# The last block of a graph-attention layer: offset, scale row and store queues at the end of the kernel

## Chip, cores and metric

One core of one Trainium2 chip. The metric is the device time of one execution in microseconds (us). A trace gives the profiled span as well, which is about 1.8 us shorter than the timed figure of the same execution. Lower is better. Engines: PE is TensorE (matmuls), DVE is VectorE, ACT is ScalarE, POOL is GpSimd, SP is SyncE, which here only issues transfers (DMA).

## The reference, cut to what matters

```python
# x: (128, 64, 768) f32, adj: (128, 64, 64); two layers l; H = 768
h = max(layernorm(x), 0)
for l in range(2):
    ...                                   # scores, exp, mask -> attention (64 x 64 for each of 128 graphs)
    h_lin = h @ W_lin[l].T + b_lin[l]
    ctx   = attention @ h_lin
    h     = relu((ctx - mean) / (std + 1e-3) * ln_a[l] + ln_b[l])
out = x + h
```

The change concerns the last line of the loop for l = 1 and the residual `x + h`, for the last sixteenth of the rows. The kernel has the mean taken out of `h_lin` beforehand, so that `ctx` comes centred and the deviation is the root of the sum of its squares.

## The kernel before: the parts concerned

The kernel makes four passes, two a layer. Each goes over 16 blocks of 512 rows. In the last pass a block's product with `W_lin` (15 groups of matmuls with `ts`/`ht` tiles; each group's PSUM bank, called X, Y, Z or V, is read out and added into `hl`: an *eviction*) is followed, in two halves, by the *context* matmuls (`attention @ h_lin`, into PSUM tiles `aux`) and by `finish`. A half r = 0 or 1 has two tiles k = 0, 1 of 128 rows and 768 columns. In the last block the halves of the product also run one after the other, so that the first half is finished while PE works on the second. `put(slot, f)` places the steps among the matmul groups; each engine has its instructions in a fixed order.

```python
def finish(u, r):                                        # (cut to the last pass)
    cx = context(u, r)                                   # PE: 8 context matmuls, 16 records
    ...
    for k in range(2):
        nc.scalar.activation(zs[k], cx[k], AF.Square, accum_out=ss[:, k:k + 1])
    nc.scalar.activation(sd, ss, AF.Sqrt, bias=floor, scale=1.0 / (H - 1.0))

    def inverse():                                       # 1 / (deviation + eps), both tiles at once
        nc.vector.tensor_scalar_add(rs, sd, EPS_LN)
        nc.vector.reciprocal(rs, rs)
    def scaled(k):
        nc.vector.scalar_tensor_tensor(zs[k], cx[k], rs[:, k:k + 1], rows["a"], op0=ALU.mult, op1=ALU.mult)
        nc.gpsimd.tensor_add(zs[k], zs[k], rows["b"])
    def done(k):
        nc.vector.scalar_tensor_tensor(xs[k], zs[k], 0.0, xs[k], op0=ALU.max, op1=ALU.add)
        for h in range(PAIR):
            nc.sync.dma_start(out[...], xs[k][...])      # two stores of 192 KB
        if k and (u < NB - 1 or r == 0):
            residual(u + r, 1 - r)                       # loads the next rows of x, just in time
...
# last block: the block before it is finished in these slots, then its own first half
linear(u, (0,), 0, {0: ((u - 1, 0), (12, 13, 15, 19, 21)), 11: ((u - 1, 1), (34, 35, 36, 42, 44))}, (1,))
linear(u, (1,), 30, {4: ((u, 0), (50, 51, 52, 56, 58))}, ())
for f in finish(u, 1):                                   # the last half: nothing beside it
    f()
```

Of the kernel before, what the change touches and what calls it, by code (L numbers as in the profile page):

```python
# [10 lines left out]
F32 = mybir.dt.float32  # L11
I32 = mybir.dt.int32
AF = mybir.ActivationFunctionType
# [4 lines left out]
def kernel(  # L18
# [58 lines left out]
    def put(slot, *fs):  # L77
        plan.setdefault(slot, []).extend(fs)
# [96 lines left out]
    def put_sums_t(key, first, step, base):  # L175

        fs = sums_t(key)
        put_all(first, fs[:5], step)
        for f, s in zip(fs[5:], (21, 22, 23, 24, 25, 27)):
            put(max(base + s, first + 5 * step), f)  # L180
# [346 lines left out]
    def pass_two(l, aside):  # L527
        last = l == L - 1
        with tc.tile_pool(name=f"two{l}", bufs=2, reuse_waits="tile") as sp:
            if last:  # L530
                for name, src in (("a", ln_a), ("b", ln_b)):
                    row(name, src[l], 0, H, sp.tile([P, H], F32, name=name, bufs=1))
            AT, HL = {}, {}

            def load(u):
                if (2, l, u) not in HT:
                    load_h(2, l, u)
                AT[u] = sp.tile([P, Q, S], F32, name="at", bufs=3)
                nc.sync.dma_start(AT[u], ATT[l][u])

            def context(u, r):


                hl, at = HL[u], AT[u]
                lo, hi = slice(0, S), slice(S, P)
                cx = [ps_aux.tile([P, 2, T], F32, name="aux") for _ in range(2)]
                for n in range(2):
                    for (j, k, i) in ((lo, 0, lo), (hi, 0, hi), (lo, 1, hi), (hi, 1, lo)):
                        q = r + 2 * k
                        m = n if j == lo else 1 - n  # L550
                        nc.tensor.matmul(cx[k][i, m, :HH], at[j, q, :], hl[j, q, m * HH:(m + 1) * HH],  # L551
                                         start=True, stop=True)
                return [c[:, :, :HH] for c in cx]

            def batch(r, k, h):
                return 4 * (h if k == 0 else 1 - h) + r + 2 * k

            XS = {}

            def residual(u, r):  # L560
                XS[u, r] = [sp.tile([P, H], F32, name="xr", bufs=4) for _ in range(2)]
                for k in range(2):
                    for h in range(PAIR):
                        nc.sync.dma_start(XS[u, r][k][h * S:(h + 1) * S], x[u * NBB + batch(r, k, h)])

            def finish(u, r):

                cx = context(u, r)
                zs = [sp.tile([P, H], F32, name="z", bufs=4 if last else 3) for _ in range(2)]
                if last and not u and not r:  # L570
                    residual(u, r)
                two = "p (n d) -> p n d"
                ss = stat.tile([P, 2], F32, name="ss")
                sd = stat.tile([P, 2], F32, name="sd1")
                rs = stat.tile([P, 2], F32, name="rs1")
                for k in range(2):
                    nc.scalar.activation(zs[k].rearrange(two, n=2), cx[k], AF.Square, accum_out=ss[:, k:k + 1])

                nc.scalar.activation(sd, ss, AF.Sqrt, bias=floor, scale=1.0 / (H - 1.0))

                def inverse():
# [4 lines that stand above are left out]
                    if last:  # L586
                        nc.vector.scalar_tensor_tensor(  # L587
                            zs[k].rearrange(two, n=2), cx[k], rs[:, k:k + 1],
                            rows["a"].rearrange(two, n=2), op0=ALU.mult, op1=ALU.mult)
                        nc.gpsimd.tensor_add(zs[k], zs[k], rows["b"])  # L590
                        return
                    nc.scalar.activation(zs[k].rearrange(two, n=2), cx[k], AF.Copy, scale=rs[:, k:k + 1])
                    for h in range(PAIR):
                        nc.sync.dma_start(ROWS[u][batch(r, k, h)], zs[k][h * S:(h + 1) * S])

                def done(k):
                    if last:
                        xs = XS[u, r]
                        nc.vector.scalar_tensor_tensor(xs[k], zs[k], 0.0, xs[k], op0=ALU.max, op1=ALU.add)
                        for h in range(PAIR):  # L600
                            nc.sync.dma_start(out[u * NBB + batch(r, k, h)], xs[k][h * S:(h + 1) * S])
                        if k and (u < NB - 1 or r == 0):
                            residual(u + r, 1 - r)

                return [inverse] + [lambda k=k: scaled(k) for k in range(2)] + [lambda k=k: done(k) for k in range(2)]

            def linear(u, rs, base, ends, more):

                b, w = tokens_of((2, l, u)), W[l, "n"]
                if rs[0] == 0:  # L610
                    HL[u] = sp.tile([P, Q, H], F32, name="hl", bufs=2)
                hl, seen = HL[u], set()
                bank = {"X": AHEAD.pop()}
                early = {0: 3, 2: 5, 6: 9}
                for i, (s, at, t, _) in enumerate(ORDER):
                    if i in FIRST and i not in PRELOAD:
                        bank[at] = fresh(l, i, rs)
                    p = bank[at]
                    for n, r in enumerate(rs):
                        for c in range(K2):  # L620
                            nc.tensor.matmul(p[:, n], b[t][:, c, r * P:(r + 1) * P], w[s][:, c, :],  # L621
                                             start=(i in FIRST and i not in PRELOAD and n == c == 0),
                                             stop=(c == K2 - 1), skip_group_check=True)
                        if n == 0:
                            run(base + 2 * i)
                    read(p, lambda o: hl[:, o % 2 * 2 + rs[0]:o % 2 * 2 + rs[0] + len(rs), o // 2 * D:(o // 2 + 1) * D],
                         i, seen)
                    if i in early:
                        bank[FIRST[early[i]][0]] = fresh(l, early[i], rs)
                    if i == 11 and more:  # L630
                        AHEAD.append(fresh(l, 0, more))
                    if i in ends:
                        what, slots = ends[i]
                        for f, n in zip(finish(*what), slots):
                            put(n, f)
                    run(base + 2 * i + 1)

            load(0)
            for u in range(NB):
                turn = not last and u >= NB - 2  # L640
                if u + 1 < NB:
                    load(u + 1)
                    put_all(9 if u else 15, affine(2, l, u + 1))
                    put_sums_t((2, l, u + 1), 15 if u else 21, 1, 0)
                    if turn:
                        load_rows(1, 0, sp)
                        put_all(10, transpose_rows(1, 0, sp), 2)
                    if u in aside:
                        aside[u]()
                    ends = {}  # L650
                    if u:
                        ends = {0: ((u - 1, 0), (6, 7, 8, 11, 12)), 7: ((u - 1, 1), (20, 21, 22, 30, 30))}
                    linear(u, (0, 1), 0, ends, (0, 1) if u + 2 < NB else (0,))
                    for n in sorted(plan):
                        plan[n - 30] = plan.pop(n)
                else:
                    if turn:
                        load_h(1, 1, 0)
                        put_all(22, affine(1, 1, 0))
                        put_sums_t((1, 1, 0), 30, 2, 30)  # L660
                    linear(u, (0,), 0, {0: ((u - 1, 0), (12, 13, 15, 19, 21)),
                                        11: ((u - 1, 1), (34, 35, 36, 42, 44))}, (1,))
                    linear(u, (1,), 30, {4: ((u, 0), (50, 51, 52, 56, 58))}, ())
                    for n in sorted(plan):
                        run(n)
                    for f in finish(u, 1):
                        f()

    def one_aside(l):
# [46 lines left out]
```

## Time and profile before

| | |
|---|---|
| timed, 4 runs | 2812.39 us median (2810.76 to 2813.75) |
| profiled span | 2811.2 us |
| PE busy over the span | 98% |
| PE idle at the end | the last 13 us |

The lines are in the prediction below. In a timeline line the columns are start and length in us, engine, source line, operation, what it writes and reads, shapes, how many equal instructions in a row it merges, and, in brackets, the idle time of the engine just before and what ended it. SPq and ACTq are DMA issues from those engines' queues, whose data arrive later. PE's records overlap, so only their starts are used here.

For what follows I measure three stretches on each trace, by instructions that every version has:

- **C**: start of the second context group of the block before the last (2771.50 before).
- **A**: start of the last block's first context group (2780.05 before).
- **T**: start of the first square of the last half (2797.49 before).

### The profile page before, as it was taken

The numbers are of one execution on the slowest core, as the hardware profiler recorded it, in microseconds if no ns is written. First come the engines' busy times: TensorE is split into PE (matmuls) and PEld (weight loads), VectorE is DVE, ScalarE is ACT, GpSimd is POOL, SyncE is SP. The second block draws the span as 40 slices with busy tenths as digits, with TensorE's granted clock in tenths as the row PEclk, the third lists the DMA queues.
The fourth block names the chain that finished last, engine by engine and source line by source line (L and its number), as shares of the span: only waits on it lengthen the run. The fifth ranks groups of instructions, "written<-read, shape, count | busy, mean of one in ns | idle before, by whom it ended". The sixth has DMA issues, their size and how long they took to land.

```text
span 2811.2 us, 46104 instructions
## 1 busy us (share of the span) xinstructions
PE 2755.9 (98%) x18712; PEld 2343.6 (83%) x18712; DVE 1338.1 (48%) x2222; ACT 838.0 (30%) x1453; POOL 1189.7 (42%) x935
## 2 busy tenths in 40 slices
PE   7999999999999999999999999999999999999997
PEld 6888888888888888888778888888888888888885
DVE  6455554454444332322334434443444335666666
ACT  2122222322231244444422121112111214545443
POOL 3343333223323455565423343223322335887875
PEclk9999999999999999999999999999999999999999
DMA  5632443234322243333563432343234304555654
GB/s 156 165 76 74 100 116 78 74 96 120 79 73 76 98 159 110 99 125 105 148 159 84 119 92 74 83 117 94 74 80 118 75 25 145 159 170 160 184 161 124
DMA packets 234068, 310.80 MB, mean 111 GB/s; under 512 B 54144, under 2 KB 184448, under 8 KB 225664
## 3 DMA queue, kind: packets, MB, share of 16 engines
q1 hardware_dynamic: 233568, 307.06, 39.9%
q8 instruction: 149, 2.44, 0.4%
q10 hardware_dynamic: 288, 0.79, 0.1%
q14 instruction: 63, 0.52, 0.1%
HBM read 202.91 MB, written 104.86 MB: 109 GB/s over the span
## 4 chain that ended last, share of the span: by engine, by line
PE 94%; DVE 2%; issue 1%; DMA 1%; POOL 1%; ACT 1%; SPq 0%; DVEq 0%; ACTq 0%; POOLq 0%
PE X L356 23%; PE V L356 15%; PE X L621 12%; PE Y L356 11%; PE Z L356 8%; PE V L621 8%; PE Y L621 6%; PE aux L382 5%; PE Z L621 4%; PE aux L551 3%; POOL w_r L144 1%; DVE m L144 0%; DMA z<-z 0%; DVE wm L396 0%; DMA x<-in_x_dram 0%
## 5 line engine op out<-in xcount | busy, mean ns | idle before, releaser
L144 POOL TENSOR_TENSOR ts<-ht 128x512 f32<-128x512 f32 x441 | 585.5, 1339 | 1249.1 <-DMA ht<-h 560.8
L189 ACT ACTIVATE m<-X 128x512 f32<-128x512 f32 x256 | 152.3, 595 | 1117.8 <-PE X L356 585.9
L144 POOL TENSOR_TENSOR ts<-ht,ts 128x512 f32<-128x512 f32 x189 | 248.8, 1324 | 155.4 <-PE X L621 78.2
L144 DVE TENSOR_TENSOR m<-m,V 128x512 f32<-128x512 f32 x256 | 174.2, 681 | 272.0 <-PE V L356 272.0
L144 DVE TENSOR_TENSOR m<-m,X 128x512 f32<-128x512 f32 x256 | 163.8, 681 | 252.0 <-PE X L356 251.4
L356 PE MATMUL X<-ts,w_l 128*128 128x256 f32 x1024 | 246.6, 384 | 10.7 <-ACT m L189 5.1
L621 PE MATMUL X<-w_n,ts 128*128 128x256 f32 x1024 | 245.1, 381 | 6.0 <-ACT hl L189 5.7
L356 PE MATMUL X<-ts,w_r 128*128 128x256 f32 x1024 | 241.9, 379 | 0.0
L144 DVE TENSOR_TENSOR m<-m,Z 128x512 f32<-128x512 f32 x128 | 88.0, 688 | 322.7 <-ACT m L189 254.4
L356 PEld LDWEIGHTS X<-ts,w_l 128*128 128x128 f32 x1024 | 194.1, 192 | 43.0 <-issue 6.0
L621 PEld LDWEIGHTS X<-w_n,ts 128*128 128x128 f32 x1024 | 192.0, 190 | 37.6 <-ACT hl L189 6.3
L356 PEld LDWEIGHTS X<-ts,w_r 128*128 128x128 f32 x1024 | 192.3, 190 | 28.7
L255 ACT ACTIVATE ht<-ht,b_col,a_col 128x512 f32<-128x512 f32 x192 | 143.1, 804 | 149.2 <-DMA ht<-h 149.2
L621 PE MATMUL Y<-w_n,ts 128*128 128x256 f32 x768 | 182.9, 380 | 0.0
L356 PE MATMUL Y<-ts,w_l 128*128 128x256 f32 x768 | 181.8, 380 | 0.0
L356 PE MATMUL Y<-ts,w_r 128*128 128x256 f32 x768 | 181.4, 379 | 0.0
L189 ACT ACTIVATE hl<-X 128x512 f32<-128x512 f32 (+1 forms) x136 | 77.7, 571 | 332.8 <-PE X L621 323.2
L621 PEld LDWEIGHTS Y<-w_n,ts 128*128 128x128 f32 x768 | 146.5, 191 | 20.1
L356 PEld LDWEIGHTS Y<-ts,w_l 128*128 128x128 f32 x768 | 146.4, 191 | 20.1
L356 PEld LDWEIGHTS Y<-ts,w_r 128*128 128x128 f32 x768 | 145.9, 190 | 19.8
L590 POOL TENSOR_TENSOR z<-z,b 128x768 f32<-128x768 f32 x64 | 115.4, 1814 | 95.4 <-DVE z L587 95.4
L144 DVE TENSOR_TENSOR hl<-hl,X 128x512 f32<-128x512 f32 (+1 forms) x136 | 83.2, 653 | 146.2 <-PE X L621 144.3
(105 smaller groups left out, 4680.7 us busy)
## 6 DMA issues: line engine op xcount, KB each, us to landing
ht<-h SPq DMA_DIRECT2D x63, 1536.0 KB, 7.2
h<-xb SPq DMA_DIRECT2D x124, 384.0 KB, 6.5
z<-z SPq DMA_DIRECT2D x128, 192.0 KB, 2.8
x<-z SPq DMA_DIRECT2D x128, 192.0 KB, 8.6
xr<-in_x_dram SPq DMA_DIRECT2D x128, 192.0 KB, 3.8
out_dram<-xr SPq DMA_DIRECT2D x128, 192.0 KB, 2.6
x<-in_x_dram SPq DMA_DIRECT2D x120, 192.0 KB, 8.5
adj<-in_adj_dram SPq DMA_DIRECT2D x64, 128.0 KB, 2.7
```

The costliest lines, as they stand in the source:

```text
L144: (eng.tensor_add if sign == "+" else eng.tensor_sub)(o, a, b)
L189: nc.scalar.activation(to(o), p, AF.Copy, scale=1.0 if sign == "+" else -1.0)
L255: nc.scalar.activation(ht, ht, AF.Relu, bias=cols[1][:, c:c + 1], scale=cols[0][:, c:c + 1])
L356: nc.tensor.matmul(p[:, g], w[ORDER[i][0]][:, c, g * P:(g + 1) * P], b()[t][:, c, :], start=(new and g == c == 0), stop=(c == K2 - 1), ski ...
L382: nc.tensor.matmul(p[h * S + e:h * S + e + 32, q, e:e + 96], ht[:, c, b * S + e:b * S + e + 32], mb[:, e:e + 96], start=(c == 0), stop=(c ...
L551: nc.tensor.matmul(cx[k][i, m, :HH], at[j, q, :], hl[j, q, m * HH:(m + 1) * HH], start=True, stop=True)
L590: nc.gpsimd.tensor_add(zs[k], zs[k], rows["b"])
L621: nc.tensor.matmul(p[:, n], b[t][:, c, r * P:(r + 1) * P], w[s][:, c, :], start=(i in FIRST and i not in PRELOAD and n == c == 0), stop=(c ...
```

## The change

Intent: shorten the chain after the last matmul. relu(z·a + b) + x is rewritten as max(z·a, -b) + (x + b). The x + b is made ahead of time on GpSimd, for rows loaded early into a spare tile (*advance adds*); the multiplication by a goes ahead of the root; the maximum takes -b; the offset's GpSimd step falls away; each tile has its own root; and the last half's stores go out on two queues. Line numbers move by 52: the residual add L599 is L651 in the new file for older blocks, the offset L590 is L642, the scale L587 is L639; the new steps are L577 (advance add), L590 (square), L592 (root), L595 (scale row), L599 to L601 (eps, reciprocal, multiply and maximum), L604 (residual add) and L606 (store).

```diff
+            def last_block(u):
+                rest = big.tile([P, C, T], F32, name="ht")...           # spare tile, cut into four row tiles
+                rows["-b"] = sp.tile([P, H], F32, name="nb", bufs=1)
+                ...
+                put(1, lambda: load(0))
+                put(2, lambda: load(1))
+                put(6, lambda: nc.gpsimd.tensor_scalar_mul(rows["-b"], rows["b"], -1.0))
+                for n, slot in enumerate((23, 26, 45, 49)):
+                    put(slot, lambda xs=XS[u, n // 2][n % 2]: nc.gpsimd.tensor_add(xs, xs, rows["b"]))
+            def finish_last(u, r):
+                ...
+                for k in range(2):                                      # square and root by tile
+                    nc.scalar.activation(XS["squares"][...], cx[k], AF.Square, accum_out=ss)
+                    nc.scalar.activation(rs[k], ss, AF.Sqrt, bias=floor, scale=1.0 / (H - 1.0))
+                def gained(k):
+                    nc.vector.tensor_tensor(zs[k], cx[k], rows["a"], op=ALU.mult)
+                def scaled(k):
+                    nc.vector.tensor_scalar_add(rs[k], rs[k], EPS_LN)
+                    nc.vector.reciprocal(rs[k], rs[k])
+                    nc.vector.scalar_tensor_tensor(zs[k], zs[k], rs[k], rows["-b"], op0=ALU.mult, op1=ALU.max)
+                def done(k):
+                    nc.vector.tensor_add(xs[k], xs[k], zs[k])
+                    for h in range(PAIR):
+                        (nc.scalar if r and h else nc.sync).dma_start(out[...], xs[k][...])
+                return [gained 0, gained 1, scaled 0, done 0, scaled 1, done 1]      # abridged
...
-                        if k and (u < NB - 1 or r == 0):
+                        if k and (u < NB - 2 or r == 0):
...
+                    else:
+                        last_block(u)
...
-                    linear(u, (1,), 30, {4: ((u, 0), (50, 51, 52, 56, 58))}, ())
+                    linear(u, (1,), 30, {4: ((u, 0), (41, 43, 47, 51, 53, 56) if last else (50, 51, 52, 56, 58))}, ())
-                    for f in finish(u, 1):
+                    for f in (finish_last if last else finish)(u, 1):
```

## The prediction

> **What bounds the kernel now.** I read the page first: TensorE (PE) is busy in 98% of the span, and the chain of work that ended last lies on it for 94%.
>
> ```profile
> span 2811.2 us, 46104 instructions
> PE 2755.9 (98%) x18712; PEld 2343.6 (83%) x18712; DVE 1338.1 (48%) x2222; ACT 838.0 (30%) x1453; POOL 1189.7 (42%) x935
> ...
> PE 94%; DVE 2%; issue 1%; DMA 1%; POOL 1%; ACT 1%; SPq 0%; DVEq 0%; ACTq 0%; POOLq 0%
> ```
>
> The diff touches only the last of 16 blocks of the last pass, and the order of the built program agrees: PE has the same instructions in the same order, and the other engines differ only in their last few dozen. So at most the stretch from about 2759 us to the end can change, 52 us of 2811. Then I read the table of windows, for how far PE still runs there (columns: window, its length, busy time of PE, weight loads, VectorE (DVE), ScalarE (ACT), GpSimd (POOL), then PE's clock, DMA share, GB/s):
>
> ```profile
> 2759.00:2775.00 16.00, 15.89 (x90) 11.28 (x90) 13.36 (x20) 6.81 (x19) 10.16 (x7) 1.00 0.48 124
> 2775.00:2788.00 13.00, 12.95 (x66) 9.65 (x65) 7.34 (x16) 5.50 (x16) 3.59 (x2) 1.00 0.50 134
> 2788.00:2799.00 11.00, 8.02 (x32) 3.86 (x30) 6.43 (x10) 1.51 (x4) 3.58 (x2) 0.84 0.62 179
> 2799.00:2811.20 12.20, 0.00 (x0) 0.00 (x0) 5.69 (x6) 0.48 (x3) 3.56 (x2) 0.59 0.42 119
> ```
>
> PE is full to 2788, has holes to 2799, and does nothing in the last 12.2 us. Those 12.2 us and the holes are all there is to win. The timeline from 2788 on, by engine, shows what fills them:
>
> ```profile
> 2787.17 3.43 SPq L564 DMA_DIRECT2D xr<-in_x_dram  x4
> 2788.70 1.94 DVE L587 SCALAR_TENSOR_TENSOR z<-aux,rs,a 128x768 f32<-128x768 f32 x2
> 2792.61 1.64 DVE L599 SCALAR_TENSOR_TENSOR xr<-z,xr 128x768 f32<-128x768 f32 x1 [1.32 <-DMA xr<-in_x_dram]
> 2794.17 0.41 DVE L144 TENSOR_TENSOR hl<-hl,Z 128x256 f32<-128x256 f32 x1
> 2794.64 3.59 PE L551 MATMUL aux<-hl,at 64*64 64x384 f32 x14 [1.37 <-DVE hl L144]
> 2797.49 0.81 ACT L577 ACTIVATE z<-aux 128x768 f32<-128x768 f32 x1 [12.05 <-PE aux L551]
> 2799.21 0.30 ACT L579 ACTIVATE sd<-ss,floor 128x2 f32<-128x2 f32 x1
> 2799.54 0.17 DVE L582 TENSOR_SCALAR rs<-sd 128x2 f32<-128x2 f32 x1 [3.76 <-ACT sd L579]
> 2800.03 1.94 DVE L587 SCALAR_TENSOR_TENSOR z<-aux,rs,a 128x768 f32<-128x768 f32 x2
> 2801.19 3.56 POOL L590 TENSOR_TENSOR z<-z,b 128x768 f32<-128x768 f32 x2 [7.76 <-DVE z L587]
> 2803.03 3.41 DVE L599 SCALAR_TENSOR_TENSOR xr<-z,xr 128x768 f32<-128x768 f32 x2 [1.06 <-POOL z L590]
> 2805.59 2.42 SPq L601 DMA_DIRECT2D out_dram<-xr  x4
> ```
>
> To see: at 2792.6 the residual add of the first row-half had waited for its late load, then ran 1.64 us, and the two eviction adds that PE's last matmuls need (L144) stood behind it on DVE. After the last matmul everything is serial: squares, root, DVE scale, GpSimd offset, DVE max-add, four stores on one queue.
>
> **What the Trainium skill says.** (1) "SBUF — State Buffer", Who interferes with whom: a DVE instruction with two SBUF inputs and a GpSimd one that reads SBUF exclude each other for the whole instruction. The trace agrees. Alone, an L599 takes 0.95 us (at 2772.92); beside a GpSimd add
>
> ```profile
> 2767.94 3.58 POOL L590 TENSOR_TENSOR z<-z,b 128x768 f32<-128x768 f32 x2 [2.36 <-DVE z L587]
> 2769.91 2.42 DVE L599 SCALAR_TENSOR_TENSOR xr<-z,xr 128x768 f32<-128x768 f32 x1
> ```
>
> it takes 2.42, ending 0.81 after the add's end at 2771.52: it waited, then ran. L587, with one input in PSUM, stays at 1.01. (2) "PSUM — Partial Sum Buffer", PSUM bank collisions: two engines may not be on one bank at once, ScalarE and VectorE reads included. The built program agrees: the new scale multiplication waits for ScalarE's square of the same tile, so "beside" means beside the square of the other tile. (3) "DMA: Bandwidth & Descriptors", Issuing engines are not separate DMA queues: a second issuing engine saves only issue time. Here one store occupies SP for 0.54 us, 2.42 for four; no run yet shows the saving. (4) "TensorE: Matmul & The Clock Gate", What's actually happening: PE's clock halves after a mostly idle window of 3.4 us. The windows above show it falling to 0.84 and 0.59, and the 14 context matmul records at 2794.64 took 3.59 us where 16 took 1.52 at 2771.50.
>
> **The change, part by part.** Call T the start of the first square of the last row-half (2797.49 now).
>
> Now: two squares with their accumulator reads end at T+1.69, root to T+2.02, add and reciprocal to T+2.4, first scale T+2.54 to 3.56, first GpSimd offset T+3.70 to 5.50 (1.81 each), then L599 waits for the lock behind the second offset and ends at T+8.08 instead of about T+6.5. Stores issue at T+8.10 and each 0.62 after; the last at about T+9.98. The span ends at T+13.71, so 3.73 us (landing, 2.8 by the issue list, and closing barriers) follow the last issue.
>
> After: square 0 with its accumulator read ends at T+0.90 and its root at 1.23; square 1 starts about 1.15 and ends with its read at 2.08. The multiplication by the scale row is a tensor-tensor: 0.416 for 256 columns and 0.683 for 512 give about 0.95 for 768. It runs at T+0.95 to 1.9 for tile 0, and, held by square 1, T+2.13 to 3.08 for tile 1. Add and reciprocal take 0.48 to the start of what follows (2799.54 to 2800.03); the multiply-max, two SBUF inputs, 0.95 as an undisturbed L599: T+3.48 to 4.43. Residual add T+4.47 to 5.42, then two stores at once, on SP and on ACT. Tile 1: add and reciprocal T+5.33, multiply-max T+5.82 to 6.77, add to T+7.75, two stores at T+7.8. Plus 3.73: **T+11.5, a gain of 2.2 us**. The offset is off the path, the lock costs nothing as GpSimd is finished, and the store queue saves one issue (0.6); against it stands one more pass of DVE per tile (0.95 each).
>
> **What T does.** DVE gets more to do before T, for the first row-half is treated the same way while PE is still running: per tile three wide DVE passes in place of two, and two small ones more in all, about 2.3 us together. And GpSimd's four advance adds (1.81 each, the first two queued behind the offsets ending at 2771.52, the others behind those ending at 2783.48) fall where DVE does residual adds for the block before. By working down the DVE order with the alternating lock:
> - The second residual add, 2772.92 now, would wait for the first advance add (2772.25 to 2774.05) and end at 2774.9, not 2773.87. The eviction behind it gates a matmul at 2774.78 with 0.25 of slack: PE loses about **0.8**.
> - Around 2784 DVE has, ahead of the eviction that releases PE's group at 2786.79, two new scale multiplications (0.9 each) and two residual adds that now meet the third and fourth advance adds. The present slack is 0.44. That PE group starts near 2790.2, so **2.6 beyond the 0.8**.
> - Gained back: no wait for a load at 2792.6 (1.32), no lock there (0.7), and no pair of L587 ahead of the evictions at 2790.5 (1.94). On my count the last eviction ends at about 2796.7 to 2797.2, against 2795.78 now; if PE is at full clock then, the context group's remainder takes about 0.9 instead of 1.7, and T becomes about 2798.1: **0.6 later**.
>
> Sum: -2.2 + 0.6 = -1.6 us. Without the collisions T would be near 2795.9 and the sum -3.8; with PE at half clock at the end too, -0.9.
>
> **The rivals.** A: the advance adds cost nothing, because their loads land after the residual adds have the lock, or the lock falls more kindly; gain near 3.8, so 2809. For it: loads here land 3.8 us after issue and eight are queued at once. Against: GpSimd is idle after its offsets, and DVE is busy 13.36 of 16 us there. B: DVE becomes the bound of the last block, T moves by 2 or more, and nothing is left: 2812 to 2813. For it: the slack of 0.25 and 0.44, and a cold PE. Against: the three waits that vanish. C: the second queue does not shorten the end, since both feed the same engines and 3.73 us of landing stay: costs 0.6 of the gain. Nothing makes 2%: that is 56 us, more than the 52 touched.
>
> **Range and chances.** The timed median is 1.5 above the profiled span (2812.73 to 2811.2), and the three runs spread over 1.7. I carry the shift over. My count gives 2811.1, rival A 2809; I weigh them two to one and say **2810.4 us**, range **2808.2 to 2812.6**: A's full gain plus noise below, B's almost nothing above. Faster by 2%: 0.004; within 2%: 0.992; slower: 0.004.
>
> **What would show each step right or wrong.** Tail: from the first square of the last row-half to the end, 11.5 us instead of 13.7; no GpSimd instruction after it; last two stores issued within 0.1 us of each other on SP and ACT. Lock: residual adds of the block before, at about 2773 and 2785 to 2789, of over 1.5 us beside GpSimd adds from the last block's tile. PE: a hole before the group that now starts at 2786.79, at about 2787.5 to 2790, with the hole at 2790.5 and the load wait of 1.32 gone. Clock: whether the last context matmuls run at half speed. The prediction is wrong if T moves by more than 1.5 either way, or if the time from last issue to end is not about 3.7.

## More of the kernel before

The kernel before has one trace only, so its own stretches have no repeat. C to end is 39.70 us in the kernel before.

## The result, and the profile after

2809.28 us median of 4 runs (2808.47 to 2810.89), against 2812.39. The ratio is 0.999, with a 95% interval of 0.9973 to 1.0007. (A ratio here is the mean time of one kernel's fast runs over the mean of the other's fast runs of the same rounds, so not quite the ratio of the medians.) 2809.28 lies in the range.

The timed difference of 3.1 us is not all the change's. In these two traces the changed kernel is already 1.30 us earlier at C, where PE's work has not changed yet. From C to the end it takes 37.51 us in place of 39.70: **2.19 us less**, which is what has to be explained. About 0.7 of it hangs on PE's clock in the one trace of the kernel before (see T under "Why the prediction was right"). Two rows of the table of windows of the changed kernel, over stretches of the prediction's:

```profile
2775.00:2788.00 13.00, 10.49 (x55) 7.47 (x53) 8.81 (x14) 5.43 (x15) 8.87 (x5) 1.00 0.38 115
2788.00:2799.00 11.00, 6.82 (x36) 4.55 (x36) 8.60 (x18) 2.28 (x6) 0.00 (x0) 1.00 0.45 109
```

GpSimd (the fifth busy figure) is gone behind 2788 and busy 8.87 us ahead of it, 3.59 before. PE now has a hole already between 2775 and 2788 (10.49 busy, 12.95 before), and its clock is 1.00 from 2788 to 2799, 0.84 before. The tail, from the timeline of the changed kernel:

```profile
2795.86 0.81 ACT L590 ACTIVATE hl<-aux 128x768 f32<-128x768 f32 x1 [11.72 <-PE aux L551]
2796.79 0.96 DVE L595 TENSOR_TENSOR z<-aux,a 128x768 f32<-128x768 f32 x1 [2.08 <-ACT hl L590]
...
2797.90 0.96 DVE L595 TENSOR_TENSOR z<-aux,a 128x768 f32<-128x768 f32 x1 [0.16 <-ACT hl L590]
...
2799.16 1.02 DVE L601 SCALAR_TENSOR_TENSOR z<-z,sd_e,nb 128x768 f32<-128x768 f32 x1
2800.28 0.96 DVE L604 TENSOR_TENSOR ht<-ht,z 128x768 f32<-128x768 f32 x1
...
2801.27 2.88 ACTq L606 DMA_DIRECT2D out_dram<-ht  x2
...
2802.66 0.96 DVE L604 TENSOR_TENSOR ht<-ht,z 128x768 f32<-128x768 f32 x1
```

From 2796.79 on DVE works with hardly a break. The last store is issued at 2803.65, when the last L604 is done: 7.79 us after T, as worked out (7.8). The end comes at T + 11.85, not 11.5. The middle, where GpSimd's third and fourth advance adds meet the residual adds under *the lock*, as the prediction calls it (one engine waits until the other's instruction is done):

```profile
2782.13 4.29 POOL L577 TENSOR_TENSOR ht<-ht,b 128x768 f32<-128x768 f32 x2
...
2782.43 0.95 DVE L595 TENSOR_TENSOR z<-aux,a 128x768 f32<-128x768 f32 x1
...
2783.30 1.46 DVE L651 SCALAR_TENSOR_TENSOR xr<-z,xr 128x768 f32<-128x768 f32 x1
...
2785.55 1.69 DVE L651 SCALAR_TENSOR_TENSOR xr<-z,xr 128x768 f32<-128x768 f32 x1
2787.16 0.74 DVE L144 TENSOR_TENSOR hl<-hl,X 128x256 f32<-128x256 f32 x2
...
2787.95 1.13 PE L673 MATMUL X<-w_n,ts 128*128 128x256 f32 x4 [2.51 <-DVE hl L144]
```

The two L651, 0.95 us each when alone, take 1.46 and 1.69, the two advance adds together 4.29 where two take 3.6. L595, which reads one operand from PSUM, is not touched. PE's group waits 2.51 us for the evictions behind them. And the place of the first advance add, where the prediction expected a loss of 0.8:

```profile
2770.20 1.52 PE L551 MATMUL aux<-hl,at 64*64 64x384 f32 x16
...
2771.62 0.95 DVE L651 SCALAR_TENSOR_TENSOR xr<-z,xr 128x768 f32<-128x768 f32 x1
2771.84 4.19 POOL L577 TENSOR_TENSOR ht<-ht,b 128x768 f32<-128x768 f32 x2 [1.62 <-DMA ht<-in_x_dram]
```

GpSimd was free from 2770.22 but waited 1.62 us for its rows. When they came, DVE's residual add was already running, and GpSimd was the one that waited.

### The profile page after: what moved, and what is told of

It reads as the page before. It is cut to its first block, busy times and chain, and to the rows that moved or that the text cites. A ratio compares the mean times of both kernels' runs of the same rounds, so it can differ in the third digit from the quotient of the medians.

```text
span 2807.7 us, 46101 instructions
## 1 busy us (share of the span) xinstructions
PE 2752.7 (98%) x18712; PEld 2342.3 (83%) x18712; DVE 1341.3 (48%) x2230; ACT 840.2 (30%) x1455; POOL 1193.7 (43%) x936
## 4 chain that ended last, share of the span: by engine, by line
PE 94%; DVE 2%; issue 1%; POOL 1%; DMA 1%; ACT 1%; SPq 0%; ACTq 0%; DVEq 0%; POOLq 0%
PE X L356 23%; PE V L356 15%; PE X L673 12%; PE Y L356 11%; PE Z L356 8%; PE V L673 8%; PE Y L673 6%; PE aux L382 5%; PE Z L673 4%; PE aux L551 3%; POOL w_r L144 1%; DVE m L144 0%; DMA z<-z 0%; DVE w_l L144 0%; DVE wm L396 0%
## 5 line engine op out<-in xcount | busy, mean ns | idle before, releaser
L144 DVE TENSOR_TENSOR hl<-hl,V 128x512 f32<-128x512 f32 (+1 forms) x136 | 89.2, 656 | 129.1 <-PE V L673 128.8
```

The lines of the kernel that those rows point to most:

```text
L144: (eng.tensor_add if sign == "+" else eng.tensor_sub)(o, a, b)
```

## The experiments

All gave correct results, and none was in a known slow state; runs without timed rounds are of unknown state, which is one reason why I compare the stretches, not the totals. All lengths in us, from each run's trace:

| kernel | C to A | A to end of last eviction | A to T | T to end | C to end |
|---|---|---|---|---|---|
| before | 8.56 | 15.72 | 17.43 | 13.71 | **39.70** |
| changed | 8.55 | 15.95 | 17.11 | 11.85 | **37.51** |
| again | 8.55 | 15.96 | 17.11 | 11.85 | 37.51 |
| one_queue | 8.55 | 15.95 | 17.10 | 11.79 | 37.44 |
| offset_back | 8.55 | 14.69 | 15.84 | 12.38 | 36.77 |
| scale_after | 8.55 | 15.96 | 17.11 | 12.32 | 37.99 |
| add_at_once | 9.49 | 15.91 | 17.05 | 11.85 | 38.39 |
| adds_early | 9.50 | 14.95 | 16.10 | 11.71 | 37.31 |
| tail_only | 9.48 | 15.98 | 16.96 | 11.84 | 38.28 |
| late_half | 8.93 | 13.64 | 14.66 | 11.71 | 35.31 |
| gained_late | 8.92 | 15.46 | 16.61 | 11.71 | 37.24 |
| late_gpsimd | 8.94 | 13.25 | 14.27 | 11.71 | **34.93** |

In the last five rows the marker A itself comes 0.25 early: its context group starts, waits within itself and takes 2.43 in place of 2.17. Against the other rows, their C to A is 0.25 short and their columns from A are 0.25 long; C to end is not touched.

### again: the changed kernel, unaltered

> The changed kernel once more, unaltered. From the first context matmul of the last block to the end the profile before has 31.15 us (2780.05 to 2811.2), the profile after 28.95 (2778.75 to 2807.7). Theory (the change acts only behind that matmul): 28.95 again within 0.4, while the place of that matmul moves freely from run to run, so that the 1.3 us by which it came earlier in the first profile does not recur as such. Timed: 2.2 below the kernel before, plus or minus 0.8. Rival (the change also speeds up what lies ahead, by 1.3): the matmul again at about 2778.8, timed gain 3.5.

Measured: C to end 37.51, to the hundredth. The first context group of the last block stood at 2780.94, where the same program had it at 2778.75: 2.2 us of drift between two executions of one kernel, all of it ahead of the change. Timed, 2811.67 median (6 runs, 2808.73 to 2818.43) against 2814.99 of the kernel before (11 runs, 2810.88 to 2819.36), ratio 0.9991, interval 0.9977 to 1.0005. So the earlier arrival of 1.3 us is not the change's doing, and the timed medians, 3.1 and 3.3 apart, cannot resolve a gain of 2.2. The stretches can.

### one_queue: all stores on the SP queue

```diff
-  (nc.scalar if r and h else nc.sync).dma_start(out[...], xs[k][...])
+  nc.sync.dma_start(out[...], xs[k][...])
```

> All stores on the SP queue. Theory (the second queue saves one issue time at the end): the last store is issued 0.55 to 0.6 us later, T to the end is 12.4 us in place of 11.84 (T is the start of the first square of the last row-half). Rival (both queues feed the same engines, so the end is set by the data): T to the end stays within 0.2 of 11.84.

Measured: the last store is issued at T + 8.30, 0.51 later than with two queues; but from the last issue to the end it takes 3.50 in place of 4.06. T to end is 11.79, against 11.85. The rival holds: the second queue is worth nothing here. In these runs the two stores issued at once landed later by as much as the issue had saved. That is so for this chain, whose two tiles are done 2.4 us apart. In the old tail they are done 0.87 apart, and there four stores on one queue, 0.62 each, are late: the last one is issued 1.03 after the last residual add ends (T + 9.97 and T + 8.94). No run has the old steps with two queues and nothing else changed.

### offset_back: last half with the old steps, rows still loaded early

```diff
-  for n, slot in enumerate((23, 26, 45, 49)):
+  for n, slot in enumerate((23, 26)):            # no advance adds for the last half
...
+  if r:   # last half: eps, reciprocal, scale from PSUM on DVE, + b on GpSimd; then max and add on DVE
+      return [old 0, old 1, old_done 0, old_done 1]      # abridged
```

> Last row-half alone: the offset is put back on GpSimd after the scale, with the old three steps (scale from PSUM after the root, GpSimd add, max and add); rows still loaded early, roots per tile, two store queues. Working it like the prediction: first scale T+1.75 to 2.7, GpSimd adds T+2.85 to 4.65 and 4.65 to 6.45, first residual add held by the lock to end at T+7.25, second at T+8.15, end at T+12.2. Theory (the lock and the GpSimd pass cost little once the roots come per tile and the stores go on two queues): 12.2, only 0.4 more than 11.84. Rival (moving the offset off the path is most of the tail's gain): 13.3 or more.

Measured: T to end 12.38, near the 12.2 of the theory and far from 13.3. Its tail:

```profile
2801.87 1.02 DVE L597 SCALAR_TENSOR_TENSOR z<-aux,sd_e,a 128x768 f32<-128x768 f32 x1
...
2803.03 3.56 POOL L599 TENSOR_TENSOR z<-z,b 128x768 f32<-128x768 f32 x2 [15.30 <-DVE sd_e L595]
...
2804.87 3.41 DVE L602 SCALAR_TENSOR_TENSOR ht<-z,ht 128x768 f32<-128x768 f32 x2 [0.60 <-POOL z L599]
```

GpSimd's second add runs until 2806.59, and the first of the two L602 waits for it under the lock: 3.41 for both, where two take 1.82 undisturbed (2783.73 in the kernel before). So the new steps save only 0.53 of the tail over the old ones. This run takes back two things at once, the offset and the place of the scale row; scale_after, the next run, parts them. And the half that it does not show in the tail: without the third and fourth advance adds, T comes 1.27 earlier. As the change stands, the new steps of the last half with their advance adds cost more than they bring: this run is 0.74 shorter than the changed kernel.

### scale_after: last half, scale row multiplied after the root

```diff
+  def at_once(k):                                # eps, reciprocal, then from PSUM:
+      nc.vector.scalar_tensor_tensor(zs[k], cx[k], rs[k], rows["a"], op0=ALU.mult, op1=ALU.mult)
+      nc.vector.tensor_max(zs[k], zs[k], rows["-b"])
...
+  if r: return [at_once 0, done 0, at_once 1, done 1]    # abridged
```

> Last row-half alone: the scale row is multiplied after the root, together with the reciprocal, straight from PSUM, then maximum and add as two more passes. The same number of wide DVE passes, but none beside the squares. Theory (DVE passes in a row set the tail, the overlap with the squares is worth little because the first pass must wait for square 0 and the second for square 1): T to the end 11.8 to 12.1. Rival (the overlap saves one pass): 12.7 or more.

Measured: 12.32, 0.47 more than 11.85. Just above the theory's band and well short of the rival's. The multiplication beside the squares is worth half a wide pass: DVE is the bound of the tail with three wide passes a tile, and the overlap only lets it start earlier (T + 0.93 in place of T + 1.26). Against offset_back, which also scales after the root, this run has the offset off the path, and the tail is 0.05 shorter (12.32 to 12.38). So of the 0.53, the offset alone brings 0.05 and the scale row beside the squares 0.47: one more DVE pass a tile costs about what GpSimd's pass did.

### add_at_once: a GpSimd add that waits for no load

```diff
-  put(6, ... tensor_scalar_mul(rows["-b"], rows["b"], -1.0))
+  put(6, ... tensor_scalar_mul(rows["-b"], rows["b"], -2.0))
+  put(22, ... tensor_add(rows["-b"], rows["-b"], rows["b"]))
```

> The negated offset row is built in two GpSimd steps (minus two b, then plus b), the second standing right behind the two offset adds of the block before and waiting for no load. It tests the step of the prediction by which the first advance add holds up a residual add and costs the matmuls 0.8 us; in the changed kernel that add came 1.6 us too late to do it, its load landing after 5.2 us, not 3.8. Theory (the lock step is right, only the landing was off): the second residual add of that stretch takes 1.9 us in place of 0.95, and from the context group of the block before to that of the last block 9.35 us pass in place of 8.55. Rival (no such slack exists or the lock falls to DVE first): 8.55.

Measured: C to A 9.49, 0.94 more than 8.55. The timeline (the file has one line more, so L651 is L652 here and the advance add L578):

```profile
2768.92 2.53 POOL L576 TENSOR_TENSOR nb<-nb,b 128x768 f32<-128x768 f32 x1
...
2770.36 1.91 DVE L652 SCALAR_TENSOR_TENSOR xr<-z,xr 128x768 f32<-128x768 f32 x1
2771.41 4.29 POOL L578 TENSOR_TENSOR ht<-ht,b 128x768 f32<-128x768 f32 x2
...
2773.07 1.10 PE L674 MATMUL V<-w_n,ts 128*128 128x256 f32 x4 [0.69 <-DVE hl L144]
```

The residual add takes 1.91, as expected for a wait behind the add, and PE stops for the eviction behind it. The step of the prediction was right; what was wrong was that the rows would be there in time.

### adds_early: all four advance adds in one row

```diff
-  for n, slot in enumerate((23, 26, 45, 49)):
+  for n, slot in enumerate((23, 26, 27, 29)):
```

> The third and fourth advance add are put right behind the first two, so that none stands beside the residual adds at 2783 to 2787. Theory (those two collisions delay the matmuls by 1.27 us, as the run with the offset put back had it): the residual adds take 0.95 each in place of 1.46 and 1.69, T comes 15.85 us after the last block's first context matmul in place of 17.11, the end 27.7 in place of 28.95. Rival (DVE's extra passes alone make the delay): 28.9.

Measured: both residual adds take 0.95 and A to T falls to 16.10, which with A's 0.25 taken off is the 15.85 expected. But C to A grows to 9.50, and C to end is 37.31: almost nothing won, so on the total the rival's number was nearer, if not for its reason. The expectation did not look for where the adds would go instead:

```profile
2774.53 7.12 POOL L577 TENSOR_TENSOR ht<-ht,b 128x768 f32<-128x768 f32 x4 [2.80 <-DMA ht<-in_x_dram]
...
2778.54 1.37 DVE L634 TENSOR_SCALAR rs<-sd 128x2 f32<-128x2 f32 x1
...
2780.14 1.94 DVE L639 SCALAR_TENSOR_TENSOR z<-aux,rs,a 128x768 f32<-128x768 f32 x2
...
2781.21 2.43 PE L551 MATMUL aux<-hl,at 64*64 64x384 f32 x16 [0.88 <-DVE z L639]
```

L634 adds eps to a tile of two columns; it has one SBUF tensor input and takes 0.17 us in the prediction's timeline (as L582). Here it takes 1.37 and ends at 2779.91, where GpSimd's third add ends (each of the four takes 1.78, so 2779.87): it, too, waits for the lock. The prediction had looked only for DVE instructions with two SBUF inputs. The scales behind L634 free the PSUM tiles that PE's context group needs, so the wait goes straight to PE (0.88).

Here is the exception to the repeatable stretches: where all four adds stand in a row, C to A depends on when the rows land. GpSimd waited 2.80 us for them in this run and C to A is 9.50; late_half, with the same adds in the same order, waited 1.50 and has 8.93. The totals of runs with early adds are therefore good to about 0.6, their stretches from A on are not touched.

### tail_only: as adds_early, with the first half in the old steps

```diff
-  (finish_last if last and what[0] == NB - 1 else finish)(*what)
+  finish(*what)
-  (41, 43, 47, 51, 53, 56) if last else (50, 51, 52, 56, 58)
+  (50, 51, 52, 56, 58)
```

> As the run before it, but the first row-half is finished by the old steps in their old places (rows still loaded early). Theory (treating the first row-half in the new way costs PE little or nothing, because what it adds on DVE ahead of the group it holds is paid back by not having two scales and the lock ahead of the last evictions): last eviction ends 15.7 after the first context matmul, as in the kernel before, T at 17.1 to 17.4, end 29.0 to 29.3. Rival (the new finish only helps in the tail, and harms in the first row-half): T below 15.8, end below 27.7.

Measured: A to T 16.96 and A to end 28.81; with the first half in the new steps (adds_early) they are 16.10 and 27.81. The rival is refuted: far from harming, the new steps in the first half bring T forward by 0.86 once the collisions are set apart. The theory's sense holds, that they cost nothing, and its numbers for T and the end, from 17.1 and 29.0 up, were 0.14 and 0.19 too long; the last eviction came 15.98 after A, not 15.7, because A came 0.25 early. A side result: the rows of this half were loaded early here, and yet its first residual add ended where it ends in the kernel before. Its line, against the L599 at 2792.61 in the prediction's timeline (the two traces stand within 0.02 us of each other from 2780.5 to 2790.9, so clock times can be compared):

```profile
2791.70 2.54 DVE L651 SCALAR_TENSOR_TENSOR ht<-z,ht 128x768 f32<-128x768 f32 x1 [0.41 <-POOL z L642]
2794.16 0.41 DVE L144 TENSOR_TENSOR hl<-hl,Z 128x256 f32<-128x256 f32 x1
```

It starts 0.9 earlier and takes 0.9 longer: the lock held it until GpSimd's second offset was done. The wait for the load, 1.32 us in the old trace, was hidden behind the lock all along. A second side result, on the clock, stands under "Why the prediction was right".

### late_half: advance adds early; first half's second tile finished behind the last eviction

```diff
-  for n, slot in enumerate((23, 26, 45, 49)):
+  for n, slot in enumerate((23, 26, 27, 29)):
-  (41, 43, 47, 51, 53, 56) if last
+  (41, 43, 47, 51, 60, 61) if last
```

> Advance adds early, and the first row-half's last maximum and residual add moved behind the last eviction, where DVE idles 2.1 us until the first square is done. Theory (DVE is the bound between the first context group and the last eviction, and this work fits in its idle stretch): T at 14.4 after the first context matmul, T to the end 11.95, end 26.4. Rival (PE or ScalarE takes over as the bound, or the moved work delays the tail by its own 2.2 us): end 27.5 or more.

Measured: T 14.66 after A (14.4 expected), T to end 11.71, A to end 26.38 (26.4 expected). C to end 35.31, 2.2 less than the changed kernel and 4.4 less than the kernel before (0.7 of this may be the clock). DVE idled 2.08 us between the last eviction and the first square's end, as the bracket at 2796.79 above shows; the maximum and residual add of one tile fit there. Timed: 2807.66 median (4 runs) against 2812.26, ratio 0.9981, interval 0.9965 to 0.9998.

### gained_late: only the order on DVE altered

```diff
-  for n, slot in enumerate((23, 26, 45, 49)):
+  for n, slot in enumerate((23, 26, 27, 29)):
-  (41, 43, 47, 51, 53, 56) if last
+  (47, 47, 47, 51, 53, 56) if last
```

> Advance adds early, and the first row-half's two scale-row multiplications moved behind the evictions that release PE's group. Theory (DVE's sum of work is the bound up to the last eviction, so the order within it is free): that PE group starts 6.7 to 7.0 us after the last block's first context matmul in place of 8.20, and T stays at 16.1. Rival (PE's hole ahead of that group is the bound): T comes earlier by what the group gains, 14.7 or less.

Measured: the PE group starts 7.00 after A (8.20 in adds_early), 1.20 sooner, but the last eviction ends at 15.46 in place of 14.95 and T comes at 16.61, 0.5 later. So the rival is refuted: PE's hole ahead of that group is not the bound. The theory is right in kind but not that order is free: with the multiplications moved, DVE stands idle for 0.43 us waiting for PE's group that the next eviction reads, where in adds_early it multiplied; most of the 0.5 at the end is this.

### late_gpsimd: late_half, with the first half's residual adds on GpSimd

```diff
   (the two edits of late_half, and)
-  nc.vector.tensor_add(xs[k], xs[k], zs[k])
+  (nc.vector if r else nc.gpsimd).tensor_add(xs[k], xs[k], zs[k])
```

> As the run with the moved half, and the first row-half's two residual adds given to GpSimd, which is idle there (its adds then stand beside evictions and multiplications with one input in PSUM). Theory (each wide pass taken off DVE ahead of the last eviction brings T forward by its 0.87 us, until PE binds at about 12.7): T 13.8 after the first context matmul in place of 14.66, from the context group of the block before to the end 34.4 in place of 35.31. Rival (the lock, or the tail's own order, takes it back): 35.2 or more.

Measured: T at 14.27 (13.8 expected, 14.66 in late_half), C to end 34.93 (34.4 expected). Half of the 0.87 came: behind the first gated group PE now runs through without a hole, and binds. From the timeline:

```profile
2787.63 1.13 PE L673 MATMUL X<-w_n,ts 128*128 128x256 f32 x4 [1.26 <-DVE sd_e L599]
...
2788.59 1.03 PE L673 MATMUL Y<-w_n,ts 128*128 128x256 f32 x4
...
2789.03 1.82 POOL L604 TENSOR_TENSOR ht<-ht,z 128x768 f32<-128x768 f32 x1 [5.63 <-DVE z L601]
...
2789.46 1.03 PE L673 MATMUL V<-w_n,ts 128*128 128x256 f32 x4
...
2791.18 1.03 PE L673 MATMUL V<-w_n,ts 128*128 128x256 f32 x4
```

GpSimd's add at 2789.03 takes its plain 1.82: beside it DVE only evicts from PSUM. From 2788.59 on PE's groups follow each other every 0.86 to 0.87 us. (The bracket names L599, the last DVE instruction before the start; what the group needs is the eviction of X.) This is the best version: 4.77 us less than the kernel before from C to the end, of which 0.7 may be the clock. Timed 2807.96 median (5 runs, 2807.01 to 2810.18) against 2813.21 (9 runs), ratio 0.9985, interval 0.9972 to 0.9999. The timed runs do not separate it from late_half.

## Why the prediction was right

**The bound.** Only what lies behind C could change; there the change takes 2.19 us off, of a predicted 1.6. The timed 2809.28 lies in the range, 1.1 below the point, and about as much is drift ahead of C (1.30 in the profiled pair; 2.2 between two executions of one kernel). That the point came so near is partly luck: the tail gained 0.34 less than predicted and T came 0.92 earlier than predicted, and the two misses work against each other; 0.73 of T may be the clock's chance (below). Of the prediction's own signs of being wrong, T did not move by more than 1.5, but from last issue to end it is 4.06 and not "about 3.7".

**The tail: 2.2 predicted, 1.86 measured.** The chain was right instruction by instruction: last store issued at T + 7.79 (7.8), no GpSimd behind T, the two last stores issued within 0.01 us of each other on SP and ACT. Mis-sized was the term "3.73 us (landing, 2.8 by the issue list, and closing barriers) follow the last issue": it measures 4.06 with two queues and 3.50 with one. So the statement that "the store queue saves one issue (0.6)" fails: it saves 0.51 of issue and pays 0.56 in landing. On this point rival C was right, for this chain. "The offset is off the path" was right too, but on its own it is worth 0.05; the overlap of the scale row is worth 0.47. The other 1.33 came with steps that offset_back kept. Its trace and that of the kernel before show where: the last residual add ends 0.81 sooner after T (8.13 in place of 8.94; each tile has its own root, and the first scale starts at 1.72 in place of 2.54), the last store follows it at once and not after 1.03, and from last issue to end it takes 4.22 in place of 3.74. The early rows bring nothing here: ahead of its last residual adds the old kernel waited for GpSimd, not for a load. No run takes the root by tile or the second queue out of the old tail alone, so this split is read from traces and not tested.

**T: predicted 0.6 later, measured 0.32 earlier.** Here the terms are:

- "PE loses about 0.8" at the first advance add: 0. The failed step is the time at which its rows arrive. I had the 3.8 us of the issue list for loads; the eight loads in a row took

```profile
L571 SPq DMA_DIRECT2D ht<-in_x_dram x8: 477/595/1110, 2765.8 to 2770.7; - x8
...
DMA to landing us min/median/max: 4.6/5.2/5.4
```

  (view of line L571 in the changed kernel). A median of 5.2. With an add that waits for no load the loss appears, 0.94.
- "2.6 beyond the 0.8" at the group behind the third and fourth adds: 2.46 (9.20 after A in place of 6.74). Of these 1.25 are the lock (7.95 in offset_back), the other 1.21 the new passes on DVE.
- The last eviction: expected at 2796.7 to 2797.2, 0.9 to 1.4 later than before; measured 0.23 later. That is the 0.8 that did not occur. In the list of what is "gained back", the load wait of 1.32 counts only together with the lock: with early rows alone the add ended where it had (tail_only), and the changed kernel takes away both.
- The rest of the context group, "if PE is at full clock then": 0.9 expected, 1.15 measured, against 1.71 before. The clock stayed at 1.00 there, and the 16 context records took 2.08 us. So the 0.32 by which T came earlier is all clock: up to the last eviction the changed kernel is 0.23 later, behind it 0.56 faster.

That clock may be chance in the one trace of the kernel before. tail_only runs PE's last part as the kernel before does: its trace has the last eviction's end at 2795.77, the other at 2795.78. The same stretch of both, first before, then tail_only (columns as in the prediction's table of windows):

```profile
2794.60:2796.50 1.90, 1.86 (x8) 0.66 (x12) 1.18 (x2) 0.00 (x0) 0.00 (x0) 0.50 0.54 126
2794.60:2796.50 1.90, 1.54 (x12) 0.54 (x13) 1.17 (x2) 0.00 (x0) 0.00 (x0) 1.00 0.57 139
```

At clock 0.50 PE did 8 records there, at 1.00 it did 12, and T came at 2797.49 and 2796.76, 0.73 apart. By this estimate the kernel before would take 38.97 from C to end with tail_only's clock, and the change would gain 1.46 in place of 2.19, with T 0.41 later. The time at which the clock falls differs from run to run: scale_after had 0.50 from 2793.3 to 2796.6 and add_at_once from 2789.1 to 2792.4, while their A to T, 17.11 and 17.05, hardly differs from the 17.11 of the changed kernel. Whether the kernel before always meets the low clock just ahead of T, and the changed one never, no run shows.

**Rival A** ("their loads land after the residual adds have the lock") was the truth for the first advance add and not for the third and fourth, whence a result between the two sums, -1.6 and -3.8. **Rival B**, DVE as the bound of the last block, was right about the bound and wrong about the price: late_half and late_gpsimd show that work taken off DVE ahead of the last eviction brings T forward, until PE binds.

## What to carry to other kernels

Taking a step off the last chain by doing it ahead of time on GpSimd is not free: look at which DVE instructions it will stand beside, small tensor-scalars included, and what waits behind those. Where DVE is the bound, look for the place where it idles in the chain (here 2.08 us while ScalarE squares) and move work there, or give work to an engine beside instructions that do not share its port. And for a few us in some thousands, measure a stretch between two instructions that all versions have; whole runs drift more than the gain. Look at the granted clock in that stretch too, and take more than one trace of each kernel: here one low-clock stretch in a single trace is a third of the gain.

## What the Trainium skill lacked or had wrong

- "DMA: Bandwidth & Descriptors", Issuing engines are not separate DMA queues: the issue time that a second issuing engine saves need not reach the end. In the new tail 0.51 us of issue were saved and the time from last issue to end grew from 3.50 to 4.06 us. The page does not say that.
- "SBUF — State Buffer", Who interferes with whom: right where it was tried. It says that tensor-scalar instructions can take both ports and then contend, which the prediction overlooked; it does not warn that this holds for the smallest of them. One of 128x2 waited 1.2 us (1.37 in place of 0.17). Nor does it say who comes next after a release; in these traces the two engines took turns, and a residual add between advance adds waited for the rest of one add and no more (1.46, 1.69, 1.91).
- "TensorE: Matmul & The Clock Gate", What's actually happening: it has an idle window halve the clock ("mostly idle" is the prediction's own word) and does not say how much work that window may hold. In the kernel before, the clock was 0.50 from 2794.3 on although PE shows 1.92 us busy in the 3.3 us ahead of it (ends modelled).
- No page that I used gives the landing time of loads issued in a row: eight of 192 KB behind four others took 5.2 us each in the median, where the kernel's like loads take 3.8.
